# Bias rows of 16 differences per head, projected in two column halves of TensorE, in a MetaFormer kernel

## The chip, the cores and the metric

The kernel runs on one core of one Trainium2 chip. The metric is the device time of one execution in microseconds (us); the times given are medians of several runs, and the profile is of one execution. All data is float32.

## The reference, cut to what matters

The input `x` is 2 x 128 x 256 x 256. The layer adds a windowed attention to the channel-normalized input and then a mixture of eight experts to the result. Only the attention's bias is touched here:

```
attn = q . k                      # 4 heads of 32 channels; window 8x8, keys from a 12x12 halo
attn = attn + rel_pos_emb(q, rel_height, rel_width) + FIXED_MASK
attn = softmax(attn);  out = attn . v
```

`rel_pos_emb` adds `q . rel_height[row difference] + q . rel_width[column difference]`. `FIXED_MASK` is minus infinity wherever the table index of either difference is even. Because of it, queries and keys split into four planes by the parity of their row and column, each window of a plane holds 4x4 queries and 6x6 keys, and of the 23 entries of each table only every second one, 9 per direction, is ever used.

## The kernel before

**Tiling.** A strip is 8 image rows of one image; there are 64 strips of four parity planes, so 256 planes. A plane holds 512 queries: 4 rows (`PR`) by 128 columns, that is 16 windows per half and two halves, or 32 groups of 4 columns. Beside a plane's attention the loop works on one "row" of the experts: 512 pixels, eight products of 128x128 by 128x512.

**The loop.** One pass of `for n in range(n_planes + 7)` (L779) interleaves, in an order written out by hand (`manual_schedule`, so each engine executes exactly this order): the scores of plane n (`scores`), the projections of plane n+1 (`project`), the attention of plane n (`attend`, `out_project`), half of the norms of two rows, and the experts of an earlier row (`Experts`). On PE (TensorE, the matmul engine) one pass is: bias matmuls L448, query-key matmuls L465, half of v L369, `pu` L384, keys `pk` L396, queries `pq` L418, four expert products L686, sums L486 and products L496 of the attention, norms L554, the other half of v L369, three expert products, `po` L524, one expert product.

**The bias.** `wrel` (L193 to L196) is the query projection times the two relative tables: per head 32 columns, of which 9 are row differences, 9 column differences and the rest zero. `pu` (L384) is one matmul of 128x128 by 128x512 that gives, per head, 32 rows of such dot products for every query. DVE (VectorE) transposes it in 32x32 blocks (`uT`, L386). `shift` (L343 to L355) then copies for each query 6 of the 9 row differences and 6 of the 9 column differences, those which its position selects, into `auT`, and transposes back into `au`: 32 rows per head, 6 + 6 used, one row of -1e30 for what lies outside. `scores` adds it to the scores by 16 matmuls (L448) of the constant `keys` (32 rows, 64 key places) by `au`.

**Instruction blocks of PE.** At the head of each pass from n = 6 on stands `nc.tensor.addr_align(BLOCK, offset=BLOCK - FIRST_LIMIT)` (L793). It fills PE's instruction stream with no-operations until the address is `FIRST_LIMIT` = 95 instructions short of the next multiple of `BLOCK` = 256, so that the limits of the blocks lie at instructions 95, 351 and 607 of each pass. Every float32 matmul is two pairs of a weight load and a matmul (four instructions).

**Queues.** All steady DMA transfers are issued by SP: gates to DRAM (`gd`) and back, spread over all partitions (`rb`, `sb`, eight `gb` per row), the input `xt` and the output. ACT (ScalarE) evacuates PSUM, squares and exponentiates.

The softmax here doesn't subtract the row's maximum and nothing guards it: scores larger than these inputs give would overflow.

## Time and profile before

| | |
|---|---|
| time, median of 3 runs | 4486.05 us (4485.24 to 4489.12) |
| span of the profiled execution, granted clock | 4480.1 us, 0.997 |
| busy: PE, DVE, ACT, POOL | 99%, 89%, 33%, 29% |
| DMA packets | 828.12 MB, 185 GB/s |

A pass takes 17.165 us in the median of the passes 20 to 239. The time on PE from the first matmul of one group to the first of the next, median of the same passes:

| group, in order | instructions | us |
|---|---|---|
| L448 bias to scores | 64 | 0.487 |
| L465 query-key | 256 | 1.459 |
| L369 half of v | 16 | 0.995 |
| L384 `pu` | 4 | 0.864 |
| L396 keys, L418 queries | 8 | 0.857 + 0.861 |
| L686 four products | 16 | 3.524 |
| L486, L496 attention | 288 | 0.456 + 1.268 |
| L554 norms | 64 | 1.011 |
| L369 other half of v | 16 | 0.995 |
| L686 three products, L524, L686 one | 20 | 2.578 + 0.858 + 0.952 |

The table is read as a budget of PE: the groups add up to the pass. In the profile a group of instructions is given as `line engine operation out<-in shapes xcount | busy us, mean ns of one | idle before`; "PEld" is PE's weight loads, which run beside the matmuls. Durations of matmuls overlap, so starts are compared rather than durations.

### The profile page before, as it was taken

How to read it: one execution, taken by the hardware profiler on the slowest of the kernel's cores; microseconds unless marked ns; L12 is line 12 of the kernel's file. 1: busy time of each engine (PE TensorE's matmuls, PEld its weight loads, DVE VectorE, ACT ScalarE, POOL GpSimd, SP SyncE). 2: the span in 40 equal slices, each digit the busy share in tenths (PEclk: the TensorE clock that was granted, in tenths of full speed). 3: DMA queues.
4: the chain of work that ended last, by engine and by line, in shares of the span. 5: the costliest groups of instructions: out<-in, count | busy, mean ns of one | idle time of the engine just before them, and what ended most of it. 6: DMA issues, size and time to landing. Idle time of an engine off the chain costs nothing. (4 is left out here: it accounts for less than half of the span.)

```text
span 4480.1 us, 224632 instructions
## 1 busy us (share of the span) xinstructions
PE 4422.6 (99%) x96321; PEld 2683.3 (60%) x96321; DVE 3996.2 (89%) x11850; ACT 1467.7 (33%) x4022; POOL 1317.7 (29%) x1815
## 2 busy tenths in 40 slices
PE   7999999999999999999999999999999999999997
PEld 5666666666666666666666666666666666666653
DVE  5899999999899999998989999999999999989887
ACT  3333333333333333333333333333333333333321
POOL 1232323232323233232323232323232323232321
PEclk9999999999999999999999999999999999999999
DMA  2565666566656666666666566666665666566655
GB/s 83 174 191 185 192 185 192 186 191 185 193 184 192 185 191 187 189 188 188 189 187 189 187 190 185 193 183 193 184 193 185 192 185 192 186 191 186 190 164 186
DMA packets 519284, 828.12 MB, mean 185 GB/s; under 512 B 124186, under 2 KB 125850, under 8 KB 518298
## 3 DMA queue, kind: packets, MB, share of 16 engines
q1 hardware_dynamic: 517568, 813.46, 58.3%
q8 instruction: 769, 12.60, 1.1%
q14 instruction: 217, 1.78, 0.2%
q10 hardware_dynamic: 730, 0.29, 0.0%
HBM read 737.95 MB, written 75.56 MB: 182 GB/s over the span
## 5 line engine op out<-in xcount | busy, mean ns | idle before, releaser
L686 PE MATMUL acc<-xe,ew 128*128 128x512 f32 x4096 | 1889.0, 594 | 19.6 <-DVE gb L660 18.8
L686 PEld LDWEIGHTS acc<-xe,ew 128*128 128x128 f32 x4096 | 758.8, 190 | 885.7 <-issue 861.8
L677 DVE TENSOR_TENSOR xe<-xs,gb 128x512 f32<-128x512 f32 x1536 | 950.9, 687 | 10.2 <-PE acc L686 0.7
L681 POOL COPY last<-xe 128x1 f32<-128x1 f32 x256 | 47.9, 187 | 3060.8 <-DVE gb L660 3054.6
L376 ACT COPY vv<-pvv 128x512 f32<-128x512 f32 x512 | 299.8, 586 | 1395.7 <-PE pvv L369 1379.6
L677 POOL TENSOR_TENSOR xe<-xs,gb 128x512 f32<-128x512 f32 x512 | 650.8, 1272 | 5.9 <-PE att L496 2.5
L369 PE MATMUL pvv<-wt,xcol 128*128 128x128 f32 x4096 | 594.3, 288 | 2.5 <-POOL xcol L331 1.5
L369 PEld LDWEIGHTS pvv<-wt,xcol 128*128 128x128 f32 x4096 | 496.4, 191 | 64.8 <-issue 51.8
L272 POOL TENSOR_TENSOR xn<-xt,rb 128x512 f32<-128x512 f32 x249 | 375.0, 1506 | 66.5 <-DMA rb<-gd 55.9
L465 PE MATMUL att<-qs,kcol 32*64 32x32 f32 x32768 | 392.4, 226 | 0.8 <-issue 0.7
L465 PEld LDWEIGHTS att<-qs,kcol 32*64 32x64 f32 x32768 | 391.0, 130 | 1.0 <-issue 1.0
L496 PEld LDWEIGHTS att<-pT,vv 64*32 64x32 f32 x32768 | 348.0, 105 | 39.4 <-issue 2.5
L496 PE MATMUL att<-pT,vv 64*32 64x32 f32 x32768 | 343.2, 200 | 2.3 <-issue 2.3
L473 ACT ACTIVATE pT<-att 128x1024 f32<-128x1024 f32 x256 | 261.9, 1023 | 243.1 <-PE att L465 239.7
L548 ACT ACTIVATE sq<-xt 128x512 f32<-128x512 f32 x505 | 292.7, 631 | 0.0
L354 DVE STREAM_TRANSPOSE au<-auT 128x512 f32<-128x512 f32 x256 | 269.2, 1052 | 9.0
L524 PE MATMUL po<-o,wt 128*128 128x512 f32 x512 | 262.0, 593 | 6.1 <-DVE o L516 3.2
L384 PE MATMUL pu<-xn,wrel 128*128 128x512 f32 x512 | 262.5, 594 | 0.0
L407 ACT COPY kcol<-pk 128x560 f32<-128x560 f32 (+2 forms) x344 | 174.1, 506 | 268.2 <-PE pk L396 265.3
L418 PE MATMUL pq<-xn,wt 128*128 128x512 f32 x512 | 262.0, 593 | 0.0
L396 PE MATMUL pk<-xn,wt 128*128 128x512 f32 (+2 forms) x528 | 261.0, 578 | 0.0
L386 DVE STREAM_TRANSPOSE uT<-pu 128x512 f32<-128x512 f32 x256 | 182.8, 714 | 78.0 <-PE pu L384 77.0
(2697 smaller groups left out, 5243.8 us busy)
## 6 DMA issues: line engine op xcount, KB each, us to landing
gb<-gd SPq DMA_DIRECT2D x2048, 256.0 KB, 4.0
xt<-in_x_dram SPq DMA_DIRECT2D x256, 256.0 KB, 4.9
sb<-gd SPq DMA_DIRECT2D x256, 256.0 KB, 3.5
out_dram<-xt SPq DMA_DIRECT2D x256, 256.0 KB, 4.2
rb<-gd SPq DMA_DIRECT2D x249, 256.0 KB, 3.3
gd<-gT SPq DMA_DIRECT2D x516, 16.0 KB, 3.0
ew<-in_L_ffn_expert_w_dram SPq DMA_DIRECT2D x1, 512.0 KB, 5.0
eb<-in_L_ffn_expert_b_dram SPq DMA_DIRECT2D x1, 512.0 KB, 5.7
```

The source lines that it names most:

```text
L272: eng.tensor_tensor(xn[i % 2][:, :, :, k, 1 : PC + 1], ln1_src(i, k).rearrange("p (y j x) -> p y x j", y=2, x=2), rb.rearrange("p (y j x) ...
L354: nc.vector.transpose(au.rearrange("p m a s -> p a s m"), auT[n % 2])
L369: nc.tensor.matmul(pv[:, t * P : (t + 1) * P], lhsT=xl[:, t0 + t].rearrange("p a k -> p (a k)"), rhs=wv, start=True, stop=True,)
L376: nc.scalar.copy(vv[:, t0 : t0 + 4, :].rearrange("p t c -> p (t c)"), pv)
L384: nc.tensor.matmul(pu, lhsT=wrel, rhs=inner, start=True, stop=True)
L418: nc.tensor.matmul(pq, lhsT=wq, rhs=inner, start=True, stop=True)
L465: nc.tensor.matmul(sc[rows, h, 32 * t : 32 * t + 32], lhsT=kk[hp, half * HP + t, :], rhs=qs[hp, m0 : m0 + 2].rearrange("p m a s -> p (m a ...
L496: nc.tensor.matmul(av[hp, half, 32 * t : 32 * t + 32], lhsT=vv[rows, t, hp], rhs=pT[rows, h, 32 * t : 32 * t + 32], start=True, stop=True,)
L524: nc.tensor.matmul(po, lhsT=wo, rhs=state["o"].rearrange("p f z -> p (f z)"), start=True, stop=True)
L548: nc.scalar.activation(sq, src, AF.Square)
L677: eng.tensor_tensor(self.xe[e], self.xs, self.gb.pop(e), ALU.mult)
L686: nc.tensor.matmul(self.acc, lhsT=ew[:, e, :], rhs=self.xe.pop(e), start=(e == 0), stop=not self.xe)
```

## The change

A softmax doesn't change when the same number is added to all scores of a query. So the last of the nine dot products of each direction is subtracted from the other eight (in `relbd`, once), the ninth becomes zero, and a head needs 16 rows instead of 32: all four heads fit in 64 rows. `pu` becomes two matmuls of 64 weight columns by 256 queries, one for each half of the plane's query rows, written to the two halves of the PSUM partitions. All that follows on DVE has half the columns: the transposes, and the shifted copies (four instead of two, with two small clears, since the ninth difference must read as zero). The second transpose leaves `both`, 16 rows per head and query half; `send`, new, moves it to the rows that the score matmuls need by eight transfers of 16 rows by 1 KB, issued by ACT between the squares of the norms and the attention. `scores` reads `au`, now a constant pair of buffers, in runs of 8 instead of 16 elements. `FIRST_LIMIT` goes from 95 to 101. The place of `pu` in the order, between v's half and the keys, stays.

```diff
-BLOCK, FIRST_LIMIT = 256, 95
+BLOCK, FIRST_LIMIT = 256, 101
+NB = 16
...
-            nc.vector.tensor_copy(
-                auT[n % 2][:, :, :, 6 * j : 6 * j + 6],
-                bass.AP(shifted.tensor, shifted.offset, dims),
...
+        for up, (rows, start) in enumerate(((slice(0, 64), 3), (slice(64, P), 1))):
...
+        for h in range(2):
...
+        nc.vector.memset(to[0:64, 0, :, :, 5:6], 0.0)
+        nc.vector.memset(to[:, :, 0, :, 11:12], 0.0)
+        both = work.tile([P, 2 * NP, 8], F32, tag="both", name=f"both{n}")
+        nc.vector.transpose(
+            both.rearrange("p m (a s) -> p a s m", a=2), to.rearrange("p a s h k -> p a s (h k)")
+        )
...
+    def send(n, state):
+
+        both = state.pop("both")
+        for up in range(2):
+            for h in range(HEADS):
+                r = (up * HEADS + h) * NB
+                nc.scalar.dma_start(au[n % 2][h * DH : h * DH + NB, up], both[r : r + NB])
...
-        nc.tensor.matmul(pu, lhsT=wrel, rhs=inner, start=True, stop=True)
-        uT = work.tile([P, PR, 4, 32], F32, tag="uT", name=f"uT{n}", bufs=1)
-        nc.vector.transpose(uT, pu.rearrange("p (a m s) -> p a s m", a=PR, s=4))
+        for up in range(2):
+            nc.tensor.matmul(
+                pu[up * 64 : (up + 1) * 64, 0 : NQ // 2],
+                lhsT=wrel,
+                rhs=inner[:, 2 * up : 2 * up + 2],
...
-                        sc[rows, h].rearrange("p (t w z) -> p t w z", w=2, z=16)[:, :, w],
+                        sc[rows, h].rearrange("p (t w a z) -> p t w a z", w=2, a=2, z=8)[:, :, w],
...
-                        rhs=au[hp, half * NP + w : (half + 1) * NP : 2].rearrange(
-                            "p t a s -> p t (a s)"
+                        rhs=bias[hp, :, half * NP + w : (half + 1) * NP : 2].rearrange(
+                            "p a t z -> p t a z"
...
             next(norm, None)
+            if n + 1 < n_planes:
+                send(n + 1, states[n + 1])
             next(attn, None)
```

More of the change, by code (lines that the diff above doesn't have):

```diff
@@ L183 @@
     lo = mid - 2 * (PR - 1)
-    relbd = ctile([P, P], "relbd")
+    relbd = ctile([P, HEADS * NB], "relbd")
     nc.gpsimd.memset(relbd, 0.0)
@@ L188 @@
         for j in range(2):
-            c0 = h * DH + NU * j
-            nc.vector.tensor_copy(
-                relbd[hp, c0 : c0 + NU], relT[j][hp, lo : lo + 2 * NU - 1 : 2]
+            c0 = h * NB + (NU - 1) * j
+            last_d = lo + 2 * (NU - 1)
+            nc.vector.tensor_tensor(
+                relbd[hp, c0 : c0 + NU - 1],
+                relT[j][hp, lo : last_d - 1 : 2],
+                relT[j][hp, last_d : last_d + 1].broadcast_to([DH, NU - 1]),
+                ALU.subtract,
             )
-    wrel = ctile([P, P], "wrel")
+    wrel = ctile([P, HEADS * NB], "wrel")
     pr = mm_tile("p_wrel")
-    nc.tensor.matmul(pr[:, :P], lhsT=wall[:, 0, :], rhs=relbd, start=True, stop=True)
-    nc.vector.tensor_copy(wrel, pr[:, :P])
+    nc.tensor.matmul(
+        pr[:, : HEADS * NB], lhsT=wall[:, 0, :], rhs=relbd, start=True, stop=True
+    )
+    nc.vector.tensor_copy(wrel, pr[:, : HEADS * NB])
     xn, xcol, kcol = [], [], []
@@ L208 @@
         nc.gpsimd.memset(kcol[i][:, NP - 1, KC - 1 : NK : KC], 0.0)
-    auT = []
+    auT, au = [], []
     for i in range(2):
-        auT.append(ctile([P, PR, 4, 32], f"auT{i}"))
+        auT.append(ctile([P, 2, 4, 2, NB], f"auT{i}"))
         nc.gpsimd.memset(auT[i], 0.0)
-        nc.gpsimd.memset(auT[i][:, :, :, KR + 6 : KR + 7], NEG)
+        nc.gpsimd.memset(auT[i][:, :, :, :, KR + 6 : KR + 7], NEG)
+        au.append(ctile([P, 2, 2 * NP, 8], f"au{i}"))
+        nc.gpsimd.memset(au[i], 0.0)
     def rstd(p4, k0, k1, name):
@@ L343, in shift @@
     def shift(uT, n, state):
-        for j in range(2):
-            shifted = uT[:, :, :, NU * j + 3 : NU * j + 9]
-            dims = [list(d) for d in shifted.ap]
-            dims[1 + j][0] -= 1
+        to = auT[n % 2]
+        for up, (rows, start) in enumerate(((slice(0, 64), 3), (slice(64, P), 1))):
+            src = uT[rows, :, :, start : start + 6]
+            step, block = src.ap[1][0], src.ap[2][0]
+            dims = [list(src.ap[0]), [step - 1, 2], [block // 2, 8], [1, 6]]
             nc.vector.tensor_copy(
-                auT[n % 2][:, :, :, 6 * j : 6 * j + 6],
-                bass.AP(shifted.tensor, shifted.offset, dims),
-            )
-        au = work.tile([P, 2 * NP, PR, 4], F32, tag="au", name=f"au{n}")
-        nc.vector.transpose(au.rearrange("p m a s -> p a s m"), auT[n % 2])
-        state["au"] = au
+                to[rows, :, :, :, 0:6].rearrange("p a s h k -> p a (s h) k"),
+                bass.AP(src.tensor, src.offset, dims),
+            )
+        src = uT[:, :, :, NU + 2 : NU + 8]
+        step, block = src.ap[1][0], src.ap[2][0]
+        for h in range(2):
+            dims = [list(src.ap[0]), [step, 2], [block - 1, 4], [1, 6]]
+            nc.vector.tensor_copy(
+                to[:, :, :, h, 6:12], bass.AP(src.tensor, src.offset + h * NB, dims)
+            )
+        nc.vector.memset(to[0:64, 0, :, :, 5:6], 0.0)
[3 more added lines that the diff above has]
+            both.rearrange("p m (a s) -> p a s m", a=2), to.rearrange("p a s h k -> p a s (h k)")
+        )
+        state["both"] = both
+    def send(n, state):
[4 more added lines that the diff above has]
+                nc.scalar.dma_start(au[n % 2][h * DH : h * DH + NB, up], both[r : r + NB])
     def project(n, state):
@@ L383, in project @@
         pu = mm_tile(f"pu{n}")
-        nc.tensor.matmul(pu, lhsT=wrel, rhs=inner, start=True, stop=True)
-        uT = work.tile([P, PR, 4, 32], F32, tag="uT", name=f"uT{n}", bufs=1)
-        nc.vector.transpose(uT, pu.rearrange("p (a m s) -> p a s m", a=PR, s=4))
+        for up in range(2):
+            nc.tensor.matmul(
+                pu[up * 64 : (up + 1) * 64, 0 : NQ // 2],
+                lhsT=wrel,
+                rhs=inner[:, 2 * up : 2 * up + 2],
+                start=True,
+                stop=True,
+            )
+        uT = work.tile([P, 2, 4, 32], F32, tag="uT", name=f"uT{n}", bufs=1)
+        nc.vector.transpose(uT, pu[:, 0 : NQ // 2].rearrange("p (a m s) -> p a s m", a=2, s=4))
         state["shift"] = lambda: shift(uT, n, state)
@@ L436, in scores @@
     def scores(n, state):
-        qs, kk, au = state["qs"], state["kk"], state["au"]
+        qs, kk, bias = state["qs"], state["kk"], au[n % 2]
         turn = place(n // 4, 0) // 2
@@ L752 @@
     states[0]["shift"]()
+    send(0, states[0])
     if n_planes > 1:
```

## The prediction

> **What bounds the kernel now.** I read the busy shares first, then the waits of each engine, then single passes on the timeline.

> ```profile
> PE 4422.6 (99%) x96321; PEld 2683.3 (60%) x96321; DVE 3996.2 (89%) x11850; ACT 1467.7 (33%) x4022; POOL 1317.7 (29%) x1815
> ...
> L686 PE MATMUL acc<-xe,ew 128*128 128x512 f32 x4096 | 1889.0, 594 | 19.6 <-DVE gb L660 18.8 <-DVE xt L692 0.8
> ...
> L384 PE MATMUL pu<-xn,wrel 128*128 128x512 f32 x512 | 262.5, 594 | 0.0
> ...
> q8 instruction: 769, 12.60, 1.1%
> ```

> PE is busy 99% and waits for DVE 18.8 us in all, so a pass lasts as long as PE's work: what counts is how PE starts one group after another. A 512-column matmul starts every 0.428 us although it is shown with 594 ns. The last line is the instruction fetch: 769 packets of 16 KB, three per pass of 17.165 us, 256 instructions each. Two passes around the limit of a block (the first is ordinary, the second late):

> ```profile
> 1731.47 0.19 PEld L418 LDWEIGHTS pq<-xn,wt 128*128 128x128 f32 x1 [0.24 <-issue]
> 1731.90 0.19 PEld L686 LDWEIGHTS acc<-xe,ew 128*128 128x128 f32 x1 [0.24 <-issue]
> 1732.34 0.19 PEld L686 LDWEIGHTS acc<-xe,ew 128*128 128x128 f32 x1 [0.24 <-issue]
> ...
> 3929.53 0.19 PEld L418 LDWEIGHTS pq<-xn,wt 128*128 128x128 f32 x1 [0.24 <-issue]
> 3929.95 0.19 PEld L686 LDWEIGHTS acc<-xe,ew 128*128 128x128 f32 x1 [0.24 <-issue]
> 3931.03 0.30 PEld L686 LDWEIGHTS acc<-xe,ew 128*128 128x128 f32 x2 [0.89 <-issue]
> ```

> The third load of each is instruction 351 (64 + 256 + 1 semaphore + 16 + 4 + 4 + 4 + 2), the first of a new block. Ordinarily it comes 0.43 after the one before, in the late pass 1.08. By the packets' stamps in the trace, the fetch that a pass starts after its first limit ends 3.81 us into the pass (10% over 4.20, latest 4.57). In the 31 of 216 passes with a late load it came 1.41 us after that end (1.28 to 1.61). A load may be 0.32 late free of charge, because the matmul before it streams 0.428 and a load needs 0.107; so the fetch delays this kernel only if it ends after about 4.44, in 3% of the passes.

> [...]L554, four column tiles of 128x32 with different moving data, takes 1.011 us for 32 matmuls of 0.107, so four run at once; and the first load of the full array after it

> ```profile
> 2271.19 0.40 PE L554 MATMUL plt<-sq,rw 128*32 128x128 f32 x8
> 2271.52 0.97 PEld L369 LDWEIGHTS pvv<-wt,xcol 128*128 128x128 f32 x8 [0.20 <-issue]
> ```

> starts 0.201 after the last of these eight matmuls (which starts at 2271.321), 0.094 after its 0.107 of streaming. [...]L448 shows it: its second round starts 0.160 after its first, 0.107 + 0.053. [...]Here the 16 KB `gd` takes 3.0.

> **The change, part by part.**

> *The projection.* Before, 0.864 us from the first matmul of `pu` to that of `pk`, with the loads hidden. After: 0.094 drain, 0.053 load of both halves, two rounds of 256 columns at once (0.428), 0.094 drain, 0.107 load of the full array that nothing hides: 0.776. Counted from the last matmul of v, 0.975 becomes 0.882: **0.09 gained per pass**, not the 0.43 that half the columns promise; two changes of mode, 0.35, eat the rest. Bounds: with no drain at all it would be 0.3; with the halves one after the other, 0.34 lost. I take 0.09, since L554 shows both concurrency and drain with all 128 rows in use.

> *The fetch.* Four more PE instructions for `pu`, and in the instruction order of the changed kernel four semaphore instructions stand among the first bias matmuls, because each waits for two transfers. The second limit moves to 357 = 64 + 4 + 256 + 1 + 16 + 8 + 4 + 4: from the second load of L686 to the first. That load is due one matmul earlier (0.43) and, by the gain itself, another 0.09 earlier[...]. Free delay then ends at 5.095 + 0.321 - 0.093 = 5.32 us, so a fetch that ends after 5.32 - 1.41 = 3.91 costs its excess. Applied to the 216 ends in this trace with the 31 delays, 36% of the passes lose, **0.084 us per pass** in the mean. If fetches end 0.2 earlier it is 0.03, 0.2 later 0.18. A pass needs 762 of its 768 instructions (767 in four passes), so no fourth block: 6 no-operations remain of 14.

> *DVE.* Two transposes of half the columns: 0.714 + 1.052 become about 0.36 + 0.53. Two copies of 0.207 become two of half the partitions, same length, and two shorter, with two clears of 0.06. About 0.4 less per pass. PE does not wait for DVE in a steady pass: nothing gained.

> *The transfers.* Eight on ACT per pass. They follow the squares (7.3 us into the pass), `both` is ready by then (`au` ended at 6.2). In the instruction order each takes the semaphore of one of the eight transfers before it; the sixth waits for `rb`, which leaves at 7.1 and lands 3.3 later, the last two wait for the second and third. So ACT is held until about 10.6. Behind them are a copy that paces `xt` and then the copy of v, which ACT otherwise awaits anyway:

> ```profile
> 2265.94 1.15 ACT L548 ACTIVATE sq<-xt 128x512 f32<-128x512 f32 x2
> ...
> 2272.72 0.59 ACT L376 COPY vv<-pvv 128x512 f32<-128x512 f32 x1 [5.54 <-PE pvv L369]
> ```

> 2272.72 is 12.98 into the pass, 2.4 later. The last transfer lands by some 13, PE needs it at 17.1. Cost zero; 128 packets of 1 KB against some 2000 per pass add 4% of bytes. Some `xt` loads start up to 1.8 us later and so crowd the end of the pass, which could push the fetch.

> *Bias matmuls.* Same 16, same columns, runs of 8 elements. No row of the trace has such runs; bounds 0 and a doubling (+0.43). I take 0, since runs of 16 already stream at full rate.

> *The ends.* The first alignment spends 104 no-operations in 7.81 us. The program ahead of it grows by 46 instructions and the target moves by 6, so 52 remain: 3.9 us less. The first scores start 2.6 us after the first `au`, and now await transfers: I estimate 1.5 us more. Subtractions instead of copies in `relbd`: equal.

> Sum: 250 passes of (0.093 - 0.084), 2.3 us, and 2.4 at the ends: 4486.05 - 4.7 = **4481**.

> **The rivals.**

> *The fetch is not late* (it ends some 0.2 earlier[...]): 250 x 0.06 + 2.4 = 17.6 to 23 with no loss at all, 4463 to 4468. For it: a fetch is free if it ends before 3.9, and half do. Against: nothing in the change moves the request by 0.2.

> *The fetch is later* (`xt`, gates and eight transfers crowd the engines): 0.2 later loses 0.18, net 22 us slower, 2.4 back: 4506. For it: fetch one starts anywhere from 1.36 to 3.69 in the pass, so it queues for something. Against: its start hardly follows the DMA engines' load around it in this trace.

> *No drain between modes of equal rows*: 0.3 - 0.19 per pass: 28 + 2 us, 4455. Against: L554 to L369 is such a pair.

> *Halves in turn, short runs at half rate, or a late `au`*: +85 to +110 us, 4575. Against each: L554, L448's rate, 4 us of slack.

> **How the numbers follow.** Main case 0.50 at 4481, with some 12 us around it by the delay of the fetch; fetch not late 0.20; fetch later 0.17; no drain 0.06; the last rival 0.07. The range 4456 to 4507 takes in the first three and leaves out the last rival and half of the no-drain case. Faster by over 9 us: 0.36 of the main case, 0.20 and 0.06: 0.44. Slower: a tenth of the main case, 0.17 and 0.07: 0.29. Within: 0.27.

> **What would show it.** Right: in the profile after, `pu` has matmuls of 128*64 with 256 columns, starts of two halves a few ns apart, about 0.77 us to `pk`; DVE near 3890 us busy; and the first load of L686 late in a third of the passes. Wrong: no late first load (then the gain is whole), 0.64 or more for `pu` without its drains, L448's group over 0.5, or PE waiting for `au`.

## The result and the profile after

The changed kernel takes **4537.4 us** (median of four runs, 4531.6 to 4544.3) against 4485.7 us before on the same chip: a ratio of 1.0116, 95% interval 1.0098 to 1.0134. It is 52 us slower. The forecast was 4481, with a range up to 4507. The experiments below ran on several chips, on which the kernel before takes 4482.9 to 4485.7 us; each ratio is against it on the same chip, and a difference of a few us between two kernels lies within the spread.

The page of the profile after, the rows that answer to those shown of before, and three new ones. The columns are those of the page before: busy us and its share, or busy us, mean ns of one, and idle time ahead with its releaser:

```profile
PE 4466.9 (98%) x96833; PEld 2684.7 (59%) x96833; DVE 3864.7 (85%) x12874; ACT 1490.6 (33%) x4022; POOL 1318.9 (29%) x1817
...
q10 hardware_dynamic: 66266, 33.97, 2.8%
q8 instruction: 769, 12.60, 1.0%
...
L727 PE MATMUL acc<-xe,ew 128*128 128x512 f32 x4096 | 1898.7, 597 | 34.7 <-DVE gb L701 17.3
...
L118 ACT COPY xt<-onesm 128x1 f32<-128x1 f32 x247 | 47.3, 192 | 1292.6 <-DMA au<-both 1262.1
```

DVE lost 132 us of work, as forecast, and PE still reads 98% busy. Two rows deserve a second look. The idle time ahead of the expert products (the old L686 is L727 now) has grown from 19.6 to 34.7 us, and of that only 17.3 is DVE's. And ACT spends 1262 us of the span behind the eight transfers `au<-both`: they are counted as idle time, so ACT's 33% does not show them. (It had idle time at this place before, too: 1379.6 us in waits for v, which the issues now fill.)

A busy PE hides what follows, so I compare starts, in the one profiled execution of each kernel (that of the changed kernel is the slowest of its four). Mean change of each group from its first matmul to that of the next, passes 16 to 235:

| group | ns per pass | forecast |
|---|---|---|
| half of v, `pu`, keys (+93, -281, +111) | -77 | -93 |
| queries, four products: late fetch (+114, +32) | +146 | +84 |
| products of the attention, L537 | +97 | 0 |
| bias, query-key, norms | +10 | 0 |
| pass, 17.171 to 17.347 us | +176 | -9 |

The start adds to this. Pass 16 starts at 305.9 us in the span instead of 284.9, 21 us later, where the forecast had all ends together at 2.4 us less. From pass 16 to the last one it is 39.9 us more, and the tail 1.4 more: 62.4, the difference of the two profiled executions (4542.5 against 4480.1).

The projection itself does what was forecast. The weight loads in an ordinary pass (start, duration, what was loaded, idle time ahead):

```profile
827.77 0.20 PEld L419 LDWEIGHTS pu<-xn,wrel 128*64 128x64 f32 x4
828.35 0.30 PEld L437 LDWEIGHTS pk<-xn,wt 128*128 128x128 f32 x2 [0.39 <-DVE g L660]
```

From the first load of `pu` to that of the keys are 0.58 us for two rounds of 256 columns, 0.214 each if a column takes what it takes in the 0.428 of 512. Both halves run at once: their matmuls start 7 ns apart in the median of the passes. If they took turns, the four would need 0.86.

A pass with a late fetch, the same group as in the two passes shown of before:

```profile
413.93 0.19 PEld L459 LDWEIGHTS pq<-xn,wt 128*128 128x128 f32 x1 [0.24 <-issue]
415.11 0.30 PEld L727 LDWEIGHTS acc<-xe,ew 128*128 128x128 f32 x2 [0.99 <-issue]
415.65 0.19 PEld L727 LDWEIGHTS acc<-xe,ew 128*128 128x128 f32 x1 [0.24 <-issue]
```

The late load is now the first of the products, as forecast: 1.18 us after the load before it instead of 0.43. In this pass (it starts at 409.35) the fetch ends 4.38 us in, and the load comes 1.38 later. Over the passes with a late load that distance is 1.40 in the mean (before 1.41). The load comes late enough to cost time, over 0.75 after the one before, in 87 of 216 passes. What is new is when fetches end. The median is still 3.8 us, but a tenth end after 4.50 (before 4.20), and the latest at 5.81 (before 4.57).

ACT in an ordinary pass (ACTq is the issuing of transfers, ACT the computing part; this pass starts at 824.73):

```profile
830.67 0.52 ACTq L389 DMA_DIRECT2D au<-both  x1
831.14 0.65 ACT L589 ACTIVATE sq<-xt 128x512 f32<-128x512 f32 x1
831.22 1.33 ACTq L389 DMA_DIRECT2D au<-both  x1
831.67 0.63 ACT L589 ACTIVATE sq<-xt 128x512 f32<-128x512 f32 x1
832.60 4.91 ACTq L389 DMA_DIRECT2D au<-both  x6
837.55 0.19 ACT L118 COPY xt<-onesm 128x1 f32<-128x1 f32 x1 [5.24 <-DMA au<-both]
837.81 0.59 ACT L410 COPY vv<-pvv 128x512 f32<-128x512 f32 x1
```

The eight issues fill 5.94 us after the pass start to about 12.8. The forecast had ACT free at 10.6. An issue takes 0.60 us in the median (0.51 to 2.38); 264 of the 2048 take over 0.7. The copy of v comes right behind the last.

### The profile page after: what moved, and what is told of

Its sections match the earlier page's. It is cut to its first block, busy times and chain, and to the rows that moved or that the text cites. A ratio compares the mean times of both kernels' runs of the same rounds, so it can differ in the third digit from the quotient of the medians.

```text
span 4542.5 us, 228329 instructions
## 1 busy us (share of the span) xinstructions
PE 4466.9 (98%) x96833; PEld 2684.7 (59%) x96833; DVE 3864.7 (85%) x12874; ACT 1490.6 (33%) x4022; POOL 1318.9 (29%) x1817
## 3 DMA queue, kind: packets, MB, share of 16 engines
q8 instruction: 769, 12.60, 1.0%
## 5 line engine op out<-in xcount | busy, mean ns | idle before, releaser
L727 PE MATMUL acc<-xe,ew 128*128 128x512 f32 x4096 | 1898.7, 597 | 34.7 <-DVE gb L701 17.3
L727 PEld LDWEIGHTS acc<-xe,ew 128*128 128x128 f32 x4096 | 752.4, 191 | 927.6 <-issue 902.9
L718 DVE TENSOR_TENSOR xe<-xs,gb 128x512 f32<-128x512 f32 x1536 | 950.6, 686 | 10.6 <-PE acc L727 1.4
L118 ACT COPY xt<-onesm 128x1 f32<-128x1 f32 x247 | 47.3, 192 | 1292.6 <-DMA au<-both 1262.1
L537 PEld LDWEIGHTS att<-pT,vv 64*32 64x32 f32 x32768 | 370.2, 105 | 44.3 <-issue 3.6
L537 PE MATMUL att<-pT,vv 64*32 64x32 f32 x32768 | 369.3, 200 | 3.4 <-issue 3.3
L437 PE MATMUL pk<-xn,wt 128*128 128x512 f32 (+2 forms) x528 | 290.7, 635 | 0.0
L547 DVE STREAM_TRANSPOSE sT<-att 128x512 f32<-128x512 f32 x256 | 183.5, 717 | 120.4 <-PE att L537 116.2
L633 ACT ACTIVATE lg<-lg 128x32 f32<-128x32 f32 x256 | 58.7, 229 | 616.0 <-DVE lg L632 616.0
L448 ACT COPY kcol<-pk 128x560 f32<-128x560 f32 (+2 forms) x344 | 174.1, 506 | 253.1 <-PE pk L437 249.5
```

Of the source, the lines that this page charges most:

```text
L437: nc.tensor.matmul(pk[:, : m * PC], lhsT=wk, rhs=xp[:, part[0] : part[0] + m, 1 : PC + 1], start=True, stop=True,)
L537: nc.tensor.matmul(av[hp, half, 32 * t : 32 * t + 32], lhsT=vv[rows, t, hp], rhs=pT[rows, h, 32 * t : 32 * t + 32], start=True, stop=True,)
L718: eng.tensor_tensor(self.xe[e], self.xs, self.gb.pop(e), ALU.mult)
L727: nc.tensor.matmul(self.acc, lhsT=ew[:, e, :], rhs=self.xe.pop(e), start=(e == 0), stop=not self.xe)
```

## The experiments

**Theory.** The projection gains what was forecast, and the transfers, costed at zero, lose more than that in three places: products of the attention that stall, first passes that wait, and instruction fetches that end later. **Rivals.** (a) The cost is in the new matmuls: the change of tile size, the short runs of the bias, their waits. (b) The block limit is in a bad place, and the transfers are innocent.

### Without the transfers, and with the limit moved

First, the transfers are taken out and nothing else. Four semaphore instructions of PE go with them, so the limit moves by four and falls on the same instruction:

```diff
-BLOCK, FIRST_LIMIT = 256, 101
+BLOCK, FIRST_LIMIT = 256, 97
...
-                nc.scalar.dma_start(au[n % 2][h * DH : h * DH + NB, up], both[r : r + NB])
```

> The changed kernel without its eight transfers per plane: the bias rows stay zero, so the scores lack the relative-position bias; all else is computed. FIRST_LIMIT is 97 instead of 101, because the four semaphore instructions are gone too, so that both block limits fall on the same matmuls as in the changed kernel. Theory 'transfers' (their issue on ACT, about 0.6 us each, makes the scores of the first planes wait and stops PE's short matmuls of the attention): the group of the attention products goes back from 1.366 to 1.27 us and the first passes lose nothing, so 4537 - 24 - 20 - 2 = 4491, and down to 4476 if the late tail of the fetch comes from them too. Rival 'matmuls' (runs of 8 elements or the changes of tiling mode cost more than counted): 4530 or more. Rival 'fetch alone': 4535.

Measured: 4466.5 us, ratio 0.9962 (0.9947 to 0.9977), so 71 us less than the changed kernel. The attention products are back at their old length (+0.1 ns), pass 16 starts at 282.1 us, and the late fetch costs 45 ns a pass instead of 146, so that the kernel is faster than any case of the expectation. v, `pu` and keys stay at -78 ns. The short runs of the bias matmuls cost nothing.

Second, the transfers stay and the limit moves ten instructions on, into the middle of the four products:

```diff
-BLOCK, FIRST_LIMIT = 256, 101
+BLOCK, FIRST_LIMIT = 256, 111
```

> The changed kernel with FIRST_LIMIT 111 instead of 101: the second block limit moves ten instructions on, from the first weight load of the four expert products to the sixth, 2.1 us later in the pass. Theory 'fetch' (a fetch that ends 1.41 us before the first instruction of a block can start costs its excess, 0.146 us per pass in the profile of the changed kernel): the loss goes, 250 x 0.146 = 36 us, so about 4500, and no late load is left. Rival 'transfers alone': 4537, nothing changes.

Measured: 4514.7 us, 1.0070 (1.0053 to 1.0086). The fetch loss is gone (queries -2 ns, products -4), worth 23 us where 36 were expected. But the attention products are not at +97 but at +129 ns, and pass 16 starts at 308.6. The limit is a third of the loss at most, so rival (b) falls.

Third, both edits:

> Both: no transfers (the scores lack the bias, all else is computed), and the second block limit at the sixth weight load of the four expert products as in the run with FIRST_LIMIT 111. If the two causes are all there is, only the projection's own gain is left, 0.077 us per pass by the profile: 4485.7 - 19 - 4 (fewer no-operations at the first alignment) = 4463. If the shorter runs of the bias matmuls or the tiling modes cost something outside their groups, it stays above 4480.

Measured: 4458.3 us, 0.9943 (0.9928 to 0.9958). A pass takes 17.081 us in the mean, 0.090 less than before. Of this, 0.081 lies in v, `pu` and keys, which is the projection's own gain; the forecast had 0.093. The rest is 0.006 of late fetches that the kernel before still had and 0.003 in the query-key group. Rival (a) falls with it as far as tile sizes and short runs go; PE's waits for the transfers are gone in this kernel, too, and are told apart by the idle transfers below.

Fourth, the changed kernel with the old limit of 95:

> The changed kernel with FIRST_LIMIT left at 95, as before the change: the second block limit falls on the second weight load of the keys, three loads (1.29 us) earlier than at 101. Theory 'fetch': a load there may start 5.32 - 1.29 = 4.03 us into the pass at the latest, the fetches end at 3.83 in the median, so 3.83 + 1.41 - 4.03 = 1.2 us are lost in nearly every pass instead of 0.146: about 1.1 x 250 = 275 us more, 4800. Rival 'fetch is no matter': 4537.

Measured: 4772.1 us, 1.0644 (1.0628 to 1.0660). The late load is now in the keys, whose group grows by 1.12 us. Six instructions are worth 235 us here: moving the limit was a needed part of the change, and it moved too little.

### What a transfer does to TensorE

To see the transfers without the change, eight that nothing reads were added to the kernel before, at the place where the changed kernel issues its own. Three versions differ in where the data lies (`keys_flat` stands here for `keys` with its last three dimensions as one, `c_keys_flat` for the same of the constant in DRAM that `keys` is loaded from):

```diff
+                nc.scalar.dma_start(ddst[h * DH : h * DH + 16, up], keys_flat[r : r + 16, 0:256])    # SBUF to SBUF
+                nc.scalar.dma_start(ddst[h * DH : h * DH + 16, up], c_keys_flat[r : r + 16, 0:256])  # DRAM to SBUF
+                nc.scalar.dma_start(dd[r : r + 16], keys_flat[r : r + 16, 0:256])                    # SBUF to DRAM
```

> The kernel before, and nothing of the change but eight transfers: ACT issues them in each pass where the changed kernel does, 16 partitions by 1 KB each, from the constant `keys` in SBUF to a tile that nothing reads. PE's instructions are those of before, and nothing on PE waits for the transfers. Theory A (each issue on ACT stops a weight load of PE's attention products about 1 us later): the group of attention products grows by 97 to 129 ns a pass as in the changed kernel, 24 to 32 us, and the fetch may lose up to 15 us more: 4505 to 4530. Theory B (the cost is PE's wait for the bias and its semaphore instructions): no stall, 4483 within 5.

> The same eight idle transfers added to the kernel before, but their source is a constant in DRAM instead of SBUF. Theory A1 (what stops PE is that ACT issues a transfer at all): as with the source in SBUF, attention products 97 to 129 ns longer a pass, 4505 to 4530. Theory A2 (what stops PE is the reading of 16 SBUF partitions): no stall, 4483 within 5.

> The kernel before with eight idle transfers per pass on ACT, as in the run at 4517.5, but from `keys` in SBUF to DRAM. Theory S (what stops PE goes with the reading of SBUF): the attention products grow as with SBUF at both ends, 60 to 130 ns a pass, 4505 to 4525. Theory B (it takes SBUF at both ends): no stall, as with the source in DRAM, 4490 to 4500.

In a fourth version SyncE issues only two, SBUF to SBUF, behind the first gate:

```diff
             new.fetch(0, dve)
+            if n + 1 < n_planes:
+                send(n + 1)      # two transfers, nc.sync
```

> The kernel before with two idle transfers per pass, SBUF to SBUF, 16 partitions by 1 KB each, issued by SyncE behind the gate `gb` of the first expert, so that one second after each issue falls into the attention products or just ahead of them. Theory A (only an issue by ACT stops PE): attention products unchanged, 4484 to 4492. Theory S (such a transfer stops PE whoever issues it): up to 0.12 us for each issue whose moment falls among these products, 50 to 200 ns a pass, 4495 to 4535.

| transfers per pass | time, us | ratio (95%) | median issue, ns | attention products, ns | four products, ns |
|---|---|---|---|---|---|
| 8 on ACT, SBUF to SBUF | 4517.5 | 1.0075 (1.0060 to 1.0090) | 547 | +78 | +36 |
| 8 on ACT, DRAM to SBUF | 4494.5 | 1.0022 (1.0012 to 1.0033) | 377 | 0 | +33 |
| 8 on ACT, SBUF to DRAM | 4493.3 | 1.0020 (1.0012 to 1.0028) | 431 | -1 | +35 |
| 2 on SP, SBUF to SBUF | 4522.3 | 1.0086 (1.0071 to 1.0101) | 546 | +147 | +4 |

The groups' rows show the same without any alignment of passes. The row of the attention products, busy us and mean ns, in the kernel before:

```profile
L496 PE MATMUL att<-pT,vv 64*32 64x32 f32 x32768 | 343.2, 200 | 2.3 <-issue 2.3
```

in the changed kernel:

```profile
L537 PE MATMUL att<-pT,vv 64*32 64x32 f32 x32768 | 369.3, 200 | 3.4 <-issue 3.3
```

with eight from SBUF to SBUF:

```profile
L505 PE MATMUL att<-pT,vv 64*32 64x32 f32 x32768 | 365.1, 200 | 2.0 <-issue 2.0
```

with eight from DRAM to SBUF:

```profile
L505 PE MATMUL att<-pT,vv 64*32 64x32 f32 x32768 | 343.4, 200 | 4.4 <-issue 4.4
```

with eight from SBUF to DRAM:

```profile
L505 PE MATMUL att<-pT,vv 64*32 64x32 f32 x32768 | 343.4, 200 | 2.6 <-issue 2.6
```

and with two on SP:

```profile
L505 PE MATMUL att<-pT,vv 64*32 64x32 f32 x32768 | 378.6, 200 | 3.2 <-issue 3.2
```

PE's instructions are the same in all of these but the changed kernel, and nothing on PE waits for the idle transfers. Yet the group's busy time grows by 22 to 35 us where the data goes from SBUF to SBUF, and not at all where one end is DRAM. So two of my expectations fell. That only an issue by ACT stops PE is refuted by the two on SP, which cost the most per transfer. That reading SBUF is enough is refuted by the transfers to DRAM.

Single passes tell the moment. In the kernel with two on SP the first issue starts 9.64 us into the pass and one weight load of the attention products comes 0.10 to 0.14 us late at 10.57 to 10.59. In 204 of the 207 such stalls (loads over 0.06 us late) in its trace the load starts 0.9 to 1.0 us after the first issue. In the changed kernel the same distance, counted from the last issue on ACT, holds for most: 84 of 117 stalls lie 0.9 to 1.1 us after one. Counted from the end of an issue it is narrower: from the 5th to the 95th percentile the stalls lie 0.38 to 0.41 us behind one, in both kernels. The loss goes with their number in passes 16 to 235: 98 stalls and 78 ns with eight idle transfers, 117 and 97 in the changed kernel, 156 and 129 with the limit at 111.

The shorter issues with DRAM at one end fall at other moments, and that could have been the reason for the zeros in the table. It is not: 72 and 70 of those issues end so that a stall 0.40 us later would fall among the attention products, and none stalls. With SBUF at both ends it is 96 of 262 (eight idle ones), 111 of 267 (changed kernel) and 207 of 212 (two on SP). Which of ACT's issues stall PE is open.

So with SBUF at both ends TensorE loses time, 78 to 147 ns a pass in the attention products. But the loss does not come with the data of these transfers: with two on SP the first packet of 1 KB on that queue starts 1.24 us or more after the first issue in each of 220 passes, and the load is late at about 0.94. The stall falls between the issue and the data. What inside the chip holds TensorE then was not found.

The last column is a second, smaller effect: with DRAM at one end nothing stalls PE, but the second limit's fetch is late more often, by 33 to 35 ns a pass, and the kernel is 9 us slower (with DRAM to SBUF 4483 within 5 was expected). All three versions with eight transfers show this; the two on SP cost 4.

### Issued by SP instead

```diff
-                nc.scalar.dma_start(au[n % 2][h * DH : h * DH + NB, up], both[r : r + NB])
+                nc.sync.dma_start(au[n % 2][h * DH : h * DH + NB, up], both[r : r + NB])
```

> The changed kernel with the block limit at 111, as in the run at 4514.7, and with SyncE's queue issuing the eight transfers instead of ACT. Theory A1 (the issue on ACT stops PE): the attention products lose their 129 ns a pass, 32 us: about 4483, or a little more if the gates' transfers behind them in that queue come late. Rival (it is the transfer's traffic, whoever issues it): the same 129 ns, moved to where SyncE issues, 4505 to 4520. If the queue holds the gates back so that VectorE waits, over 4530.

Measured: 5095.7 us, 1.1362 (1.1346 to 1.1379), the last case. SP's queue is the gates' too. The waits of GpSimd in this kernel:

```profile
POOL xn L285 <- DMA rb<-gd: 437.1, 156, 31.7
```

Before, GpSimd waited 55.9 us for `rb` in all. So this run told nothing of the stall, and that SP's issues stall PE as well had to be shown by the two idle ones.

### The start

```diff
     states[0]["shift"]()
-    send(0, states[0])
...
-            if n + 1 < n_planes:
+            if 8 <= n + 1 < n_planes:
                 send(n + 1, states[n + 1])
```

> The changed kernel (limit 101), but the transfers of planes 0 to 7 are left out, so that these eight planes lack their bias. Theory (in the first passes PE waits for transfers that ACT issues late, and pass 16 then starts 21 us later than before): pass 16 starts at 282 to 292 instead of 306, and the kernel ends 14 to 24 us earlier, 4513 to 4523. Rival (the first passes are slow for another reason, such as the transfers that crowd the loads of `x`, or the loss is made up for later): above 4530.

Measured: 4513.1 us, 1.0066 (1.0050 to 1.0083). Pass 16 starts at 284.7 us, as before, and the kernel is 24 us faster than the changed one. So the 21 us of the start are the transfers of the first eight planes. PE waits in two places there. One is the bias itself, 11 times in the first 310 us (us in total, times, longest):

```profile
PE att L489 <- DMA au<-both: 6.2, 11, 2.9
```

The other is `po`, and its chain shows in the trace of the changed kernel. ACT in the fourth pass (part of its lines):

```profile
93.17 5.31 ACTq L389 DMA_DIRECT2D au<-both  x8
98.52 0.19 ACT L118 COPY xt<-onesm 128x1 f32<-128x1 f32 x1 [5.95 <-DMA au<-both]
98.62 0.58 ACT L410 COPY vv<-pvv 128x512 f32<-128x512 f32 x1
```

and PE:

```profile
99.25 1.84 PE L565 MATMUL po<-o,wt 128*128 128x512 f32 x2 [4.45 <-ACT vv L410]
101.02 1.16 PE L489 MATMUL att<-au,keys 32*64 32x128 f32 x32
```

The first passes have no expert products: before the change the first four took about 12 us each instead of 17. The eight issues do not fit beside that. `po` needs the PSUM buffer that the copy of v frees, the copy stands behind the eighth issue, and PE stops for 4.45 us. PE also comes back slower, as the granted clock shows (its mean over the stretch is the column ahead of the DMA share; stretches of the same trace):

```profile
99.20:101.00 1.80, 1.75 (x2) 0.30 (x2) 0.49 (x3) 0.31 (x2) 0.00 (x0) 0.59 0.47 151
101.00:106.00 5.00, 5.00 (x174) 4.15 (x174) 1.16 (x3) 1.61 (x2) 0.00 (x0) 0.81 0.13 39
```

The clock is at 1.00 through the stop of 4.45 us and at half from 99.5 to 102.9 us, so the means are 0.59 and 0.81: the next pass needs 0.908 us for the bias matmuls instead of 0.488. The trace before has the same with a stop of 6.72 us (106.4 to 113.1): half clock from 108.1 to 118.4. What brings the half clock on was not shown: in the changed kernel the clock is also at half from 68.8 to 72.2 us, and PE has no stop over 1.5 us between 24.7 and there. Up to pass 16 the clock is at half for 34.1 us in the changed kernel, for 10.2 before the change and for 6.8 without the first eight planes' transfers.

### `pu` ahead of v

The price of a change of tile size was in the forecast. It can be paid once less: the scores are tiles of 32x64, `pu` of 128x64, v and keys of 128x128, so `pu` can stand between the scores and v.

```diff
-        values(0)
-        yield
         pu = mm_tile(f"pu{n}")
...
         state["shift"] = lambda: shift(uT, n, state)
         yield
+        values(0)
+        yield
```

> The changed kernel with the block limit at 111, as in the run at 4514.7, and with the two halves of `pu` ahead of v's first half, so that the tiles go 32x64 (scores), 128x64 (`pu`), 128x128 (v, keys). One change of tile size less: if each costs a drain of 0.094 and a load that nothing hides (0.053 or 0.107), as the prediction has it, 0.15 to 0.20 us a pass less, 37 to 50 us: 4465 to 4478. Rival: the change from 32x64 to 128x64 costs as much as both did, or v then waits for its copy: 4510 to 4520.

Measured: **4441.9 us**, 0.9903 (0.9886 to 0.9919), better than both kernels with the whole computation in place. v's half and the keys are back at their old lengths (0 and +5 ns) and `pu` keeps its -281: the three together now gain 276 ns, 199 more than in the changed kernel. The transfers fall elsewhere, too: the attention products are only 17 ns longer than before.

> Two edits at once: `pu` ahead of v's first half and no transfers at all (the bias is then left at zero), with the limit at 107 as in the run at 4458.3, which had no transfers either. What the order of the tiles is worth with ACT free: 4458.3 less 250 times 0.18 us, 4412 to 4416, if one change of tile size is all that it takes away. Rival (the order moves DVE's and ACT's work, and part of the gain seen with transfers came from where the transfers then fall): 4425 or more.

Measured: 4406.3 us, 0.9823 (0.9808 to 0.9838). With ACT free the order is worth 52 us against the 4458.3, or 194 ns a pass (17.081 to 16.887). So the order gains by itself, and the transfers cost 36 us in the kernel at 4441.9.

Part of these 36 was in view: in 37 of 220 passes a weight load of `po` waited longer than usual for the same copy of v as in the first passes. In 21 of them the matmuls came late, too: 36 ns a pass in the mean over all. Such a pass on ACT:

```profile
2544.27 7.78 ACTq L389 DMA_DIRECT2D au<-both  x6
2552.10 0.19 ACT L118 COPY xt<-onesm 128x1 f32<-128x1 f32 x1 [7.56 <-DMA au<-both]
2552.20 0.58 ACT L410 COPY vv<-pvv 128x512 f32<-128x512 f32 x1
```

and PE:

```profile
2552.83 1.12 PE L566 MATMUL po<-o,wt 128*128 128x512 f32 x2 [0.43 <-ACT vv L410]
```

Two edits tried to free the copy. One puts `rb` behind the eight in the program, so that none of them takes over its semaphore; the other issues the last two transfers behind the copy.

> The kernel at 4441.9 (`pu` before v, limit 111) with one more edit: in the program the transfer of `rb` comes behind the eight of the bias, so that none of these takes over `rb`'s semaphore. There, in 37 of 220 passes PE waited in `po` for a buffer that ACT's copy of v frees, queued behind the eighth transfer, 36 ns a pass in the mean. If that wait is for semaphores of SyncE's transfers, it goes: 4430 to 4436. Rival (it goes to `rb`, which now waits for the bias transfers, and GpSimd is late with the normalised rows): 4442 or more.

> The kernel at 4441.9 (`pu` before v, limit 111) with the last two of the eight transfers issued behind ACT's copy of v's second half instead of ahead of it. The copy is then never held by them, and PE's wait in `po` goes, 9 us: about 4433. Rival (these two then land after PE asks for the bias at the start of the next pass, and the wait is there): 4442 to 4480.

```diff
+            if later:                                                 # rb later
+                rb1 = spread_rb(*later, f"_{n}")
...
-                send(n + 1, states[n + 1])                            # split
+                send(n + 1, states[n + 1], range(6))
...
             next(ahead, None)
+            if n + 1 < n_planes:
+                send(n + 1, states[n + 1], range(6, 8))
```

With `rb` later: 4439.5 us, 0.9898 (0.9884 to 0.9913). The groups around `po` lose 14 ns instead of 36, the bias matmuls 15 instead of 9. The gain of 2.5 us is within the interval and below the 6 to 12 expected, so this is not settled. With the split: 4650.3 us, 1.0361 (1.0331 to 1.0391), far worse than either case of the expectation. PE now waits for the late two at the head of most passes (206 waits):

```profile
PE att L490 <- DMA au<-both: 100.1, 206, 1.8
```

The bias group is 709 ns longer. Issued behind the copy, the last two come too late for the scores.

## Why the prediction was wrong, step by step

**What bounds the kernel: right.** PE's order of starts decides, and every difference above was found there.

**The projection: right.** Forecast 0.093 us per pass, measured 0.077 to 0.081, with 0.58 from `pu` to keys. The two halves run at once and two changes of tile size eat most of the gain; taking one away returned 0.194 to 0.199. The forecast's 0.107 for a load of the full array, for which it shows no row, can be read in its late pass at 3931 us: the load behind the late one starts 0.108 after it.

**DVE: right.** 3865 us busy against 3890 forecast, and nothing gained by it.

**Bias matmuls with runs of 8: right,** zero: the four rounds start 0.160, 0.109 and 0.109 us apart in an ordinary pass, with runs of 16 before and of 8 after. The kernel without transfers has them too.

**The fetch: the mechanism right, the term mis-sized.** The limit moved to the load named, and a fetch costs what it ends after 3.91 us. That rule, applied to the ends measured in each trace, gives 0.052 us per pass without transfers (measured 0.045) and 0.164 in the changed kernel (measured 0.146; 0.102 in the kernel without the first transfers, whose later passes are the same, so the size moves from one execution to another). The forecast of 0.084 used the ends of the trace before. The prediction said that later loads could push the fetch, and kept them out of the sum; the share of ends beyond 3.91 hardly changed (36% to 39%; 24% without transfers), but the late ones became later. The rival "the fetch is later" had the cause and the size of this term (0.18), and missed the rest.

**The transfers, "cost zero": the step that failed.** It asked only whether the data lands before PE needs it. In steady passes it does. Apart from the later fetches, these were not on that path:

- Issuing. Eight transfers hold ACT for almost 7 us, 5.9 to 12.8 into the pass. The forecast had 10.6, though the trace before showed two issues of `gd` in 1.17 us; eight of those are 4.7 us before any wait. In steady passes of the changed kernel PE loses nothing by this (the groups around `po` are unchanged); in the first passes it does.
- The stall of the attention products, 97 to 129 ns a pass. Nothing in the trace before shows it, since no transfer of that kernel goes from SBUF to SBUF.
- The first passes, +21 us instead of -2.4 at the ends. The 4 us of slack were read from a steady pass of 17 us. The first passes have 12. There one of the prediction's own signs of being wrong showed: PE waiting for `au`.

Taken together the transfers cost 71 us (4537.4 less 4466.5). In the profiles of these two it is 23.9 at the start and 0.208 a pass after it: about half of that in the attention products, half in later fetches.

**The range: too narrow above.** The rival that held a late `au` was put at 4575 as a wait in every pass. A cost between it and the main case was not in the list, because the transfers had no bounds of their own: no row priced one from SBUF to SBUF, so their cost should have had an upper end. Two sums of the rival without a late fetch are off as well: 250 x 0.06 + 2.4 is 17.4, and with no loss at all it is 250 x 0.093 + 2.4 = 25.7, so 4460 to 4469 instead of 4463 to 4468. Nothing hangs on them.

## What to carry to other kernels

A transfer that lands in time is not free (the eight cost 71 us here): count its issue on the engine that sends it, name what that engine has queued behind, and look at the shortest pass, not at the steady one. Where small matmuls like these run, keep transfers with SBUF at both ends from being issued a microsecond ahead of them: two a pass on SP cost 147 ns a pass in the attention products. When a matmul gets narrower tiles, order the groups by tile size: here the place of one group was worth more than twice what its narrower tiles gained, 0.199 us a pass against 0.077.
